# First front of a four-layer hybrid: one of four convolved channel groups on VectorE, vectors in three packs, edges turned ahead of the convolution, first parts reloaded in pieces

## The chip, the cores and the metric

The kernel runs on one NeuronCore of a Trainium2 chip. A core has TensorE (PE, matrix products), VectorE (DVE), ScalarE (ACT), GpSimd (POOL) and SyncE (SP, which here issues nearly all DMAs), each with an instruction stream of its own. The metric is the device time of one execution in microseconds (us); the median of three runs is compared.

## The reference

Four layers work on x of 4 images of 32 x 32 tokens with 256 channels, in float32. Layer 0 is the one that the change touches. For each image:

```python
x = _layernorm(src, ln1_g, ln1_b)
x = x @ w_in + b_in                                  # 256 -> 512 channels
x = conv3x3_depthwise(x, conv_w, padding='SAME') + conv_b
x = gelu(x).reshape(B, L, 512)                       # L = 1024
dt_raw, Bm, Cm = split(x @ w_x, [16, 16 + 64])
dt = softplus(dt_raw @ w_dt + dt_bias)
# h[t] = exp(dt[t] * A) * h[t-1] + dt[t] * x[t] * Bm[t];  y[t] = sum_n h[t] * Cm[t]
y = scan(...) + x * D_skip
out = layernorm(y) @ w_out + b_out                   # and src is added
```

(The call of the convolution is abbreviated; it has one 3 x 3 filter for each of 512 channels.) Layer 1 is a small convolution block. Layer 2 is an attention over tokens whose mask comes from a list of 69,632 edges (source and destination token; only pairs inside the 1024 tokens count), then a mixture of 8 experts. Layer 3 is a second state-space scan (16 states instead of 64), then another mixture of experts.

## The kernel before

**The scans.** Both state-space layers are cut into units of 128 partitions (states x channels) by 1024 time steps: 256 units for each image in layer 0, 64 in layer 3, 1280 in all. The generator `scans` (L364) writes them out in the order `SCANS`: images of layer 0 come ahead of the layer-3 images that depend on them. A unit needs its decay `dA` (a broadcast load of dt from DRAM, `load` L430, then an exponential on ACT, `decay` L443), its input `ps_rep` (a product of a selection matrix with `S`, the bfloat16 parts of dt * x, `first` L453), a product with B on VectorE, the scan itself on VectorE, a product with C on POOL (tile `h`), and a sum over states on TensorE (`pair` L468). `S` is loaded for each 128 channels by `chunk` (L385), which for a new image also loads B and C as `rows`. Loads, decays and inputs are written a few units ahead; `h` has five buffers and `ps_rep` two.

**The stages beside them.** All other work is a list of stages (`STAGES`): four fronts (layer 0 up to dt, x and B, C), four middles (end of layer 0, layers 1 and 2, start of layer 3), four lasts. Each is a generator. `run` (L560) writes two half units of the scan, then lets the current stage go on for some steps, by a clock: `Metered` adds up an estimated cost of every instruction by engine, and the stage goes on only while no engine's sum exceeds VectorE's. So the order of all instructions is fixed when the program is written, by these costs, and the POOL operations count in it.

**The first front.** The first unit needs the first 128 channels of front 0, so `chunk(0)` calls `need` (L525), which writes out stage steps until they are ready. Between two steps it takes one step of `mask_work`, the generator `setup`. That one makes the tables of A (`scan_setup` L321), then the mask (`mask_prepare`: edges loaded, turned by TensorE, turned to addresses, sorted on VectorE so that the valid ones come first, 64 of each partition; the largest count decides in a branch whether more must be sorted), then the scatters: 64 DMAs of POOL, each of which clears one mask entry of each partition, then four branches on POOL for counts above 64. In the scan one step of `mask_work` is taken for each unit.

Before that, `load_vectors` (L196) loads all bias, gain and filter vectors in two packs of rows (96 and 48), each row by a DMA on SP's queue, and turns them by TensorE into columns.

In `front` (L709) the four groups of 128 channels go one after the other (`inward` L737): two matmuls of 512 columns for the input product, evacuated by ACT into a padded image of 34 x 34; nine diagonal matrices made by ACT from the filter; two halves of nine matmuls each (`ps_cv`); gelu on ACT. Then `steps` (L589) follows: for the first 128 channels `linear` and `soft` (softplus on ACT), `rows(1)` (B and C), `add`, `split`, `low` (three bfloat16 parts) and `store`. `prepare`, which folds weights of later layers, follows at the end of front 0.

Of the kernel before, what the change touches and what calls it, by code (L numbers as in the profile page):

```python
# [53 lines left out]
        ("L0_conv_conv_b", 4), ("L0_conv_dt_bias", 4), ("L0_conv_D_skip", 4), ("L0_conv_ln2_g", 4),  # L54
        ("L0_conv_ln2_b", 4), ("L1_conv_b1", 1), ("L1_conv_g1", 1), ("L1_conv_be1", 1),
        ("L1_conv_m1", 1), ("L1_conv_v1", 1), ("L1_conv_b2", 1), ("L1_conv_g2", 1),
        ("L1_conv_be2", 1), ("L1_conv_m2", 1), ("L1_conv_v2", 1), ("L2_attn_bq", 2),
        ("L2_attn_bk", 2), ("L2_attn_bv", 2), ("L3_attn_b_in", 8), ("L3_attn_b_conv", 4), ("L3_attn_b_dt", 4),
    ),
    (("L2_ffn_b1", 16), ("L3_ffn_b1", 32)),  # L60
)

# [70 lines left out]
class Hybrid:  # L133
    def __init__(self, ctx, tc, a, out):
        self.ctx, self.tc, self.nc, self.a = ctx, tc, tc.nc, a
        self.out = out.rearrange("b h w c -> (b h w) c")
        nc = self.nc
        self.const = const = ctx.enter_context(tc.tile_pool(name="const", bufs=1))
        self.dram = ctx.enter_context(tc.tile_pool(name="dram", bufs=1, space=DRAM))

        self.ident = const.tile([P, P], F32, name="ident")
        make_identity(nc, self.ident)
        self.identb = const.tile([P, P], BF16, name="identb")
        nc.vector.tensor_copy(self.identb, self.ident)

        order = const.tile([P, NEXP], I32, name="order")
        nc.gpsimd.iota(order, pattern=[[-1, NEXP]], base=NEXP, channel_multiplier=0)
        self.order = const.tile([P, NEXP], F32, name="orderf")
        nc.vector.tensor_copy(self.order, order)
        self.eps = {}  # L150
        for e in (1e-5, 1e-3):
            self.eps[e] = const.tile([P, 1], F32, name=f"eps{len(self.eps)}")
            nc.vector.memset(self.eps[e], e)

        self.x0 = const.tile([P, TB, C], F32, name="x0")
        nc.sync.dma_start(self.x0, self.image(a["x"].rearrange("b h w c -> (b h w) c"), 0))
        self.w_in0 = self.weight(const, "L0_conv_w_in", 2)
        for _ in self.norm(const, self.x0, TB, self.x0, "ln0"):
            pass

        self.blocks = const.tile([P, P], F32, name="blocks")
        make_block_diagonal(nc, self.blocks, 4)
        self.states = {0: 64, 3: 16}
        self.mem = {}
# [31 lines left out]
    def load_vectors(self):  # L196

        nc, a = self.nc, self.a
        self.vec = {}
        with self.tc.tile_pool(name="vstage", bufs=1) as sp, self.tc.tile_pool(  # L200
            name="vpsum", bufs=1, space=PSUM
        ) as pp:
            for n, pack in enumerate(VEC_PACKS):
                rows = sum(k for _, k in pack)
                stage = sp.tile([rows, P], F32, name=f"vstage{n}")
                r = 0
                for name, k in pack:
                    src = a[name]
                    if name == "L0_conv_conv_w":
                        src = src.rearrange("i j u (k p) -> (i j u k) p", p=P)  # L210
                    elif len(src.shape) == 2:
                        src = src.rearrange("e (k p) -> (e k) p", p=P)
                    else:
                        src = src.rearrange("(k p) -> k p", p=P)
                    nc.sync.dma_start(stage[r : r + k, :], src)
                    r += k
                ps = pp.tile([P, rows], F32, name=f"vps{n}")
                nc.tensor.transpose(ps, stage, self.ident[:rows, :rows])
                cols = self.const.tile([P, rows], F32, name=f"cols{n}")
                nc.vector.tensor_copy(cols, ps)  # L220
                r = 0
                for name, k in pack:
                    self.vec[name] = cols[:, r : r + k]
                    r += k
# [96 lines left out]
    def scan_setup(self, stage, name, n):  # L321
# [8 lines left out]
        flat = self.a[name].rearrange("(u g) n -> u (g n)", g=G)  # L330
        for k in range(0, units, P):
            m = min(P, units - k)
            raw = stage.tile([m, P], F32, name=f"Ar{k}_" + name)
            nc.sync.dma_start(raw, flat[k : k + m, :])
            turned = stage.tile([m, P], F32, name=f"At{k}_" + name)
            nc.vector.tensor_copy(
                turned.rearrange("u (n g) -> u g n", g=G), raw.rearrange("u (g n) -> u g n", n=n)
            )
            ps = self.early("ps_A")
            nc.tensor.transpose(ps[:, :m], turned, self.ident[:m, :m])  # L340
            nc.scalar.activation(cols[:, k : k + m], ps[:, :m], AF.Exp)
# [17 lines left out]
        return cols, spread, collect  # L359
# [4 lines left out]
    def scans(self, mp, psum):  # L364
# [20 lines left out]
        def chunk(k):  # L385

            if k >= len(units):
                return
            scan, d, c, i, j = units[k]
            if (c, i, j) != (0, 0, 0):  # L390
                return
            n = self.states[scan[0]]
            self.need(scan, d)
            if d == 0:
                bct = self.mem["bc", *scan]
                pair = []
                for t in range(2):
                    x = mp.tile([P, L], F32, tag=f"rows{t}", name=f"rows{t}", bufs=2)
                    nc.sync.dma_start(
                        x, bct[t * n : (t + 1) * n, :].unsqueeze(1).to_broadcast([n, P // n, L])  # L400
                    )
                    pair.append(x)
                rows[scan] = pair
            S = mp.tile([3 * 32, 4, L], BF16, tag="S", name="S", bufs=2)
            for s in range(3):
                nc.sync.dma_start(
                    S[32 * s : 32 * s + 32, :, :],
                    self.mem["parts", *scan, d][s].rearrange("(j p) t -> p j t", p=32),
                )
            chunks[scan, d] = S  # L410

# [85 lines left out]
        for k in range(4):  # L497
            load(k)
# [26 lines left out]
    def need(self, scan, d):  # L525

        late = False
        while ("parts", *scan, d) not in self.ready:
# [3 lines left out]
            for _ in range(SCATTERED if self.sorted else 1):  # L532
                next(self.mask_work, None)
        if late:

            self.clock.update(dict.fromkeys(self.clock, max(self.clock.values())))
# [23 lines left out]
    def run(self):  # L560
# [3 lines left out]
        self.alone = False  # L564
        nc, tc = self.nc, self.tc
        with tc.tile_pool(name="scan", bufs=1) as mp, tc.tile_pool(
            name="scps", bufs=1, space=PSUM
        ) as psum, tc.tile_pool(name="sdps", bufs=1, space=PSUM) as side, tc.manual_schedule():
            self.side_psum(side)
            self.mask_work, self.sorted = self.setup(), False  # L570
# [18 lines left out]
    def steps(self, fp, key, w, src, chunks, bias, u, between=None):  # L589
# [65 lines left out]
        if between is not None:  # L655
# [4 lines left out]
            for item in ahead:  # L660
                soft(item)
            yield from between
# [46 lines left out]
    def front(self, b):  # L709
# [3 lines left out]
        with tc.tile_pool(name=f"f{b}", bufs=1, side="right") as op:  # L713
# [4 lines left out]
            with tc.tile_pool(name=f"fa{b}", bufs=1, side="right") as fp:  # L718
# [8 lines left out]
                pads = [fp.tile([P, 34, 34], F32, name=f"pad{i}") for i in range(2)]  # L727
                for i in range(2):
                    nc.gpsimd.memset(pads[i], 0.0)
# [6 lines left out]

                def inward(item):  # L737
                    d, g, k = item
                    pad = pads[d % 2]
                    if g < 0:  # L740
# [10 lines left out]
                        )  # L751
                        if h == 0:
# [32 lines left out]
                items = []  # L785
                for d in range(DC):
                    items += [(d, -1, 0), (d, -1, 1)]
                    items += [(d, g, k) for g in range(2) for k in range(3)]
                yield from self.pipe(items, inward, cost=2.3)
            with tc.tile_pool(name=f"fb{b}", bufs=1, side="right") as fp:  # L790
# [215 lines left out]
    def mask_prepare(self):  # L1006
# [16 lines left out]
        with tc.tile_pool(name="mprep", bufs=1) as mp:  # L1023
# [15 lines left out]
            yield from [None] * 8  # L1039
# [6 lines left out]
            yield from [None] * 4  # L1046
            for a, rawf in enumerate(rawfs):
# [5 lines left out]
                yield  # L1053
# [21 lines left out]
            ps = self.early("ps_c")  # L1075
            nc.tensor.transpose(ps[:1, :P], cnt, self.ident)
            top = mp.tile([1, 1], F32, name="top")
            nc.vector.tensor_reduce(top, ps[:1, :P], AX.X, ALU.max)
            more = mp.tile([1, len(SCATTERS)], F32, name="more")
            for i, (first, _) in enumerate(SCATTERS):  # L1080
                nc.vector.tensor_scalar(more[:, i : i + 1], top, float(first), None, ALU.is_gt)
            nc.vector.tensor_copy(self.more, more)
            order = mp.tile([P, ne], F32, name="sorted")
            few = SCATTERS[0][1]
            nc.vector.memset(order[:, few:], 0.0)
# [9 lines left out]
            yield  # L1095
# [7 lines left out]
            yield  # L1103
# [3 lines left out]
        self.sorted = True  # L1107
# [724 lines left out]
    def setup(self):  # L1832
        with self.tc.tile_pool(name="prep", bufs=1) as st:
            yield
            self.tables = {}
            for scan, name, n in ((0, "L0_conv_A_log", 64), (3, "L3_attn_A_log", 16)):
                self.tables[scan] = self.scan_setup(st, name, n)
                yield
        yield from self.mask_prepare()
# [35 lines left out]
def hybrid_kernel(tc, a, out):  # L1875
    with ExitStack() as ctx:
        k = Hybrid(ctx, tc, a, out)
        k.load_vectors()
# [38 lines left out]
```

## Time and profile before

| what | value |
|---|---|
| median of 3 runs | 6605.04 us (6598.39 to 6610.3) |
| profiled execution | 6610.56 us, its span 6608.8 us |
| VectorE busy | 5140.0 us, 78% |
| GpSimd busy | 3642.9 us, 55% |
| TensorE busy | 5331.1 us, 81%, at a mean granted clock of 0.83 |
| first scan on VectorE starts | 152.63 us |
| unit 256, 512, 1024 start their scan | 1243.9, 2365.2, 4667.3 us |
| last unit starts its scan | 6168.3 us |

A span is the time from the first to the last instruction of the program. The time of a run lies 1.8 us above it. VectorE's 1280 units take most of its time (scan 2.28 us, product with B 1.21 us each); what lies ahead of the first unit has no unit under it. The lines of the profile in the prediction give start and length in us, the engine, the line of the program, the operation with its tiles, the number of instructions, and in brackets how long the engine had been idle and which engine or DMA released it. `ps_cv` is the convolution, `ps_in` the input product, `ps_e` the turned edges, `ps_c` the turned count of edges, `ps_x` the product with w_x, `ps_dt` that with w_dt. A float32 matmul is recorded as two. Line L124 is that of the recording helper, so tiles tell operations apart.

### The profile page before, as it was taken

How to read it: one execution, taken by the hardware profiler on the slowest of the kernel's cores; microseconds unless marked ns; L12 is line 12 of the kernel's file. 1: busy time of each engine (PE TensorE's matmuls, PEld its weight loads, DVE VectorE, ACT ScalarE, POOL GpSimd, SP SyncE). 2: the span in 40 equal slices, each digit the busy share in tenths (PEclk: the TensorE clock that was granted, in tenths of full speed). 3: DMA queues.
4: the chain of work that ended last, by engine and by line, in shares of the span. 5: the costliest groups of instructions: out<-in, count | busy, mean ns of one | idle time of the engine just before them, and what ended most of it. 6: DMA issues, size and time to landing. Idle time of an engine off the chain costs nothing. (4 is left out here: it accounts for less than half of the span.)

```text
span 6608.8 us, 59799 instructions
## 1 busy us (share of the span) xinstructions
PE 5331.1 (81%) x20236; PEld 2161.6 (33%) x20320; DVE 5140.0 (78%) x4310; ACT 3438.2 (52%) x4113; POOL 3642.9 (55%) x1793
## 2 busy tenths in 40 slices
PE   6667868679797568979689779898699688978979
PEld 2022312222342022234145232243255222524656
DVE  3978989988799997889889987898999971248411
ACT  3346566345477334557558445477487344245411
POOL 2857677755458665545856665556756651055200
PEclk8667868689798579979789789898699789877989
DMA  2454555643355566335645664345555750156221
GB/s 103 145 161 159 175 165 163 192 141 113 109 167 173 183 169 152 112 119 179 190 143 170 196 157 129 107 143 174 185 164 163 198 135 15 45 144 159 72 64 35
DMA packets 348113, 936.91 MB, mean 142 GB/s; under 512 B 37140, under 2 KB 119648, under 8 KB 346144
## 3 DMA queue, kind: packets, MB, share of 16 engines
q1 hardware_dynamic: 345616, 930.35, 46.3%
q0 software_dynamic: 2128, 2.13, 0.2%
q8 instruction: 172, 2.82, 0.2%
q14 instruction: 197, 1.61, 0.1%
HBM read 842.59 MB, written 93.95 MB: 142 GB/s over the span
## 5 line engine op out<-in xcount | busy, mean ns | idle before, releaser
L124 POOL TENSOR_TENSOR h<-h,rows 128x1024 f32<-128x1024 f32 x1280 | 3029.7, 2369 | 1948.9 <-DVE h L124 1736.3
L124 DVE TENSOR_TENSOR_SCAN h<-dA,ps_rep 128x1024 f32<-128x1024 f32 x1280 | 2923.9, 2284 | 169.3 <-issue 31.2
L124 DVE TENSOR_TENSOR ps_rep<-ps_rep,rows 128x1024 f32<-128x1024 f32 x1280 | 1552.8, 1213 | 254.0 <-PE ps_rep L124 253.7
L124 ACT ACTIVATE dA<-dA,A_L_conv_A_log 128x1024 f32<-128x1024 f32 x1024 | 1149.8, 1145 | 598.6 <-DMA dA<-dt 554.5
L124 PE MATMUL ps_rep<-S,spread_L_conv_A_log 96*128 96x512 bf16 x2048 | 762.1, 462 | 715.3 <-DVE h L124 694.5
L124 PE MATMUL ps_y<-h,collect_L_conv_A_log 128*32 128x512 f32 x4096 | 795.5, 759 | 70.4 <-POOL h L124 69.9
L124 PE MATMUL ps_h<-xTm,we 128*128 128x512 f32 x1536 | 717.2, 606 | 1.4 <-DVE tb L124 1.4
L124 PE MATMUL ps_e<-we,h_m 128*128 128x256 f32 x3072 | 699.3, 380 | 2.3 <-ACT h_m L124 2.3
L124 ACT ACT_TABLE_LOAD x501 | 642.8, 1283 | 52.0 <-PE ps_h L124 38.6
L124 PEld LDWEIGHTS <-spread_L_conv_A_log 96*128 96x128 bf16 x2048 | 160.7, 103 | 1489.7 <-DVE h L124 1195.1
L124 PEld LDWEIGHTS ps_e<-we,h_m 128*128 128x128 f32 x3072 | 579.9, 190 | 146.3 <-issue 45.5
L124 DVE SCALAR_TENSOR_TENSOR tb<-ps_e,cw,tb 128x256 f32<-128x256 f32 x512 | 220.7, 474 | 408.0 <-PE ps_e L124 407.6
L124 ACT ACTIVATE h_m<-ps_h,cols 128x512 f32<-128x512 f32 x384 | 260.4, 687 | 487.6 <-PE ps_h L124 484.8
L124 ACT ACTIVATE p<-ps_sc 128x512 f32<-128x512 f32 x432 | 234.4, 595 | 470.5 <-PE ps_sc L124 320.0
L124 PEld LDWEIGHTS ps_h<-xTm,we 128*128 128x128 f32 x1536 | 292.4, 194 | 338.5 <-issue 294.1
L124 ACT ACTIVATE dA<-dA,A_L_attn_A_log 128x1024 f32<-128x1024 f32 x256 | 290.5, 1146 | 199.5 <-DMA dA<-dt 164.8
L124 PE MATMUL ps_at<-p,v 128*32 128x512 f32 x1024 | 359.9, 610 | 37.8 <-ACT p L124 25.2
L124 PE MATMUL ps_rep<-S,spread_L_attn_A_log 96*128 96x512 bf16 x512 | 184.4, 448 | 177.0 <-DVE h L124 166.1
L124 PE MATMUL ps_sc<-qT,kT 32*128 32x512 f32 x864 | 249.3, 648 | 30.7 <-issue 22.9
L124 PE MATMUL ps_at<-p,ones 128*32 128x512 f32 x1024 | 271.9, 610 | 0.0
L124 PE MATMUL ps_cv<-pad,diag 128*128 128x512 f32 x576 | 262.0, 597 | 0.0
L124 PEld LDWEIGHTS ps_y<-h,collect_L_conv_A_log 128*32 128x32 f32 x4096 | 109.8, 119 | 458.5 <-issue 237.1
(327 smaller groups left out, 4916.1 us busy)
## 6 DMA issues: line engine op xcount, KB each, us to landing
dA<-dt SPq DMA_DIRECT2D x1280, 512.0 KB
we<-in_L_ffn_W_dram SPq DMA_DIRECT2D x64, 512.0 KB
parts<-parts SPq DMA_DIRECT2D x64, 384.0 KB
S<-parts SPq DMA_DIRECT2D x96, 256.0 KB
dt<-sp_r SPq DMA_DIRECT2D x64, 256.0 KB
y<-yo SPq DMA_DIRECT2D x128, 128.0 KB
y_back<-y SPq DMA_DIRECT2D x64, 256.0 KB
we<-in_L_ffn_w_dram SPq DMA_DIRECT2D x64, 256.0 KB
```

The lines of the kernel that those rows point to most:

```text
L124: return got(*args, **kw)
```

## The change

Five edits belong together.

1. `BY_VECTOR = (3,)`: in front 0 the convolution of channel group 3 is done by VectorE (`beside`): one multiplication and eight multiply-adds of 128 x 1024 over windows of its own padded image. Its input product is the first of the four; its gelu (`activate`) comes after all groups.
2. The vectors come in three packs. The first, with what front 0 needs, is loaded and turned ahead of the norm; the two others are loaded in `setup`, behind the edges and front 0's weights, ahead of the tables' raw data.
3. The edges are loaded first in `setup` and turned ahead of the convolution. Sorting is written before the count is known; count, branch and addresses (`where`) wait until the first softplus is written (`self.ahead`). `need` now ends with a loop that writes `mask_work` up to the end of this part (`self.sorted`), so scatters begin with the scan.
4. For the first `S`, six DMAs are issued by ACT, the first quarter ahead of the rest, and the first `dA` is loaded ahead of `rows`.
5. `scan_setup` is a generator: its loads are all issued first.

```diff
+BY_VECTOR = (3,)
@@ __init__
         self.w_in0 = self.weight(const, "L0_conv_w_in", 2)
+        self.vec = {}
+        first = self.load_vectors(const, 0)
         for _ in self.norm(const, self.x0, TB, self.x0, "ln0"):
             pass
+        with tc.tile_pool(name="vpsum", bufs=1, space=PSUM) as pp:
+            self.turn_vectors(0, first, pp.tile([P, P], F32, name="vps0"))
@@ chunk
+            S = mp.tile([3 * 32, 4, L], BF16, tag="S", name="S", bufs=2)
+
+            def load_parts(js, queue):
+                for s in range(3):
+                    queue.dma_start(
+                        S[32 * s : 32 * s + 32, js, :],
+                        self.mem["parts", *scan, d][s].rearrange("(j p) t -> p j t", p=32)[:, js, :],
+                    )
+
+            if k == 0:
+                load_parts(slice(0, 1), nc.scalar)
+                load_parts(slice(1, 4), nc.scalar)
+                load(0)
             if d == 0:
...
+            if k:
+                load_parts(slice(0, 4), nc.sync)
@@ need
+        while not self.sorted:
+            next(self.mask_work)
@@ steps
             for item in ahead:
                 soft(item)
+            self.ahead = True
             yield from between
@@ front
+                vector = () if b else BY_VECTOR
+                pads = [fp.tile([P, 34, 34], F32, name=f"pad{i}") for i in range(2 + len(vector))]
...
+                def beside(d, pad):
+                    to = u[:, d, :].rearrange("p (h w) -> p h w", w=32)
+                    for k in range(9):
+                        i, j = divmod(k, 3)
+                        window = pad[:, i : i + 32, j : j + 32]
+                        w = vec["L0_conv_conv_w"][:, k * DC + d : k * DC + d + 1]
+                        if k == 0:
+                            nc.vector.tensor_scalar(to, window, w, None, ALU.mult)
+                        else:
+                            nc.vector.scalar_tensor_tensor(to, window, w, to, ALU.mult, ALU.add)
+
+                def activate(d):
+                    nc.scalar.activation(
+                        u[:, d, :], u[:, d, :], AF.Gelu_apprx_tanh,
+                        bias=vec["L0_conv_conv_b"][:, d : d + 1],
+                    )
+                    nc.sync.dma_start(self.keep(("u", *key, d), [P, L]), u[:, d, :])
...
+                        if d in vector:
+                            if h == 1:
+                                beside(d, pad)
+                            return
...
+                items = [(d, -1, h) for d in vector for h in range(2)]
                 for d in range(DC):
-                    items += [(d, -1, 0), (d, -1, 1)]
-                    items += [(d, g, k) for g in range(2) for k in range(3)]
+                    if d not in vector:
+                        items += [(d, -1, 0), (d, -1, 1)]
+                        items += [(d, g, k) for g in range(2) for k in range(3)]
                 yield from self.pipe(items, inward, cost=2.3)
+                for d in vector:
+                    activate(d)
@@ mask_prepare
+            for r in range(0, few, 8):
+                largest(r)
+            while not self.ahead:
+                yield
             ps = self.early("ps_c")
             nc.tensor.transpose(ps[:1, :P], cnt, self.ident)
...
-        self.sorted = True
@@ setup
+            masks = self.mask_prepare()
+            next(masks)
+            stages = [self.load_vectors(st, n) for n in (1, 2)]
             self.tables = {}
+            tables = [
+                self.scan_setup(st, name, n) for name, n in (("L0_conv_A_log", 64), ("L3_attn_A_log", 16))
+            ]
+            for t in tables:
+                next(t)
+            yield
+            yield
+            for t in tables:
+                next(t)
                 yield
+            for n in (1, 2):
+                self.turn_vectors(n, stages[n - 1], self.early("vps"))
+            yield
+            yield from masks
+        self.sorted = True
         yield from self.scatter()
```

## The prediction

> **What bounds the kernel now.** The slices by tenths say where to look: VectorE (DVE) is 9 tenths busy from about 150 us to 5,600 us, and the first 150 us hold no scan. The chain that ended last is of no use here: it reaches back only to 5,606 us, and the change ends before that. So I read the timeline of each engine over the first 400 us. TensorE first (start, length, engine, line, operation, count, idle before and its releaser):
>
> ```profile
> 65.52 0.37 PE L124 MATMUL ps_c<-ident,cnt 128*1 128x128 f32 x1 [6.49 <-DVE cnt L124]
> 65.69 9.36 PE L124 MATMUL ps_cv<-pad,diag 128*128 128x512 f32 x18
> ...
> 112.75 7.04 PE L124 MATMUL ps_x<-u,w_L_conv_w_x 128*16 128x512 f32 x16
> 119.72 1.98 PE L124 MATMUL ps_dt<-dtr,w_dt 16*128 16x512 f32 x4
> 121.63 3.70 PE L124 MATMUL ps_x<-u,w_L_conv_w_x 128*128 128x512 f32 x8
> 128.81 5.40 PE L124 MATMUL ps_x<-u,w_L_conv_w_x 128*128 128x512 f32 x8 [3.48 <-ACT bct L124]
> 150.25 1.87 PE L124 MATMUL ps_rep<-S,spread_L_conv_A_log 96*128 96x512 bf16 x4 [16.04 <-DMA S<-parts]
> ```
>
> From 26.7 to 112.75 us TensorE is the path: four convolved groups, broken once by a wait for the edge count. After that the path is a chain over all engines, and it ends in a load. VectorE beside it:
>
> ```profile
> 79.11 0.71 DVE L1089 MATCH_REPLACE8 lin<-sorted,lin 128x544 f32<-128x544 f32 x1
> 84.50 0.45 DVE L124 TENSOR_SCALAR lin<-sorted 128x544 f32<-128x544 f32 x1 [4.68 <-issue]
> ...
> 126.53 0.69 DVE L124 SCALAR_TENSOR_TENSOR sp_e<-ps_dt,sp_e 128x512 f32<-128x512 f32 x1 [40.35 <-ACT sp_l L124]
> ...
> 137.89 1.46 DVE L124 TENSOR_TENSOR parts<-sp_x,parts 128x512 bf16<-128x512 f32 x2
> 151.29 1.23 DVE L124 TENSOR_TENSOR ps_rep<-ps_rep,rows 128x1024 f32<-128x1024 f32 x1 [11.95 <-PE ps_rep L124]
> 152.63 2.29 DVE L124 TENSOR_TENSOR_SCAN h<-dA,ps_rep 128x1024 f32<-128x1024 f32 x1
> ```
>
> It idles 40 us before 126.53, and the 4.68 us before 84.50 are the branch over the second sort. The first scan, 152.63, is where the 1280 units begin. The DMA issues between, on SP's queue:
>
> ```profile
> 138.63 1.10 SPq L648 DMA_DIRECT2D parts<-parts  x2
> 139.83 1.53 SPq L399 DMA_DIRECT2D rows<-bc  x2
> 142.49 1.30 SPq L406 DMA_DIRECT2D S<-parts  x3
> 143.83 33.37 SPq L438 DMA_DIRECT2D dA<-dt  x12
> ```
>
> Last, GpSimd (POOL) at the end of the mask's scatters, and the busy times from 152 to 321 us (PE, PEld, DVE, ACT, POOL, clock, DMA share, GB/s):
>
> ```profile
> 320.40 1.00 POOL L124 DMA_INDIRECT mask_dram<-zero,where  x1 [0.17 <-issue]
> 321.41 2.37 POOL L124 TENSOR_TENSOR h<-h,rows 128x1024 f32<-128x1024 f32 x1
> 330.03 2.36 POOL L124 TENSOR_TENSOR h<-h,rows 128x1024 f32<-128x1024 f32 x1 [6.25 <-issue]
> ```
> ```profile
> 152.00:321.00 169.00, 109.12 (x260) 14.84 (x262) 155.64 (x95) 72.50 (x77) 153.40 (x94) 0.62 0.46 148
> ```
>
> A unit costs POOL 2.36 us for h, and with a scatter 0.17 + 1.00 + 0.02 more: 3.55 us. VectorE needs 1.21 + 2.29 us and gaps: 3.54 us. While scatters run, both are full.
>
> **What the Trainium skill says.** "Runtime: NRT & Kernel Launch", Instruction fetch mechanics: a taken branch out of the fetched window waits for a DMA of the target page. The trace agrees: 4.68 us on DVE, 6.25 us on POOL at its first branch. "DMA: Bandwidth & Descriptors", Issuing engines are not separate DMA queues: queues share 16 engines, a second issuer saves issue time only. No run here has shown it yet for ACT's queue. "TensorE: Matmul & The Clock Gate", The HAM clock gate: an idle PE is throttled. The 18 matmuls after the gap took 9.36 us, 0.52 each, against 0.434 (15.62 / 36) elsewhere.
>
> **The change, step by step.** *Removed from TensorE:* one convolution, 36 records, 15.62 us; the wait for cnt with its transpose, 6.86; the slow restart, 18 x (0.52 - 0.434) = 1.5. Sum 24.0 us. The edge transposes (2 x 0.77) only move.
>
> *Added ahead of the convolution.* In the built order the A tables now stand behind two weight loads, four edge loads and 21 vector loads on SP. After the pause at 3.98 us (ends 6.36), I count 0.42 + 0.50 + 4 edge loads 1.9 + 19 x 0.295 + 0.8 and the wait for w_in until 7.61: their issue ends at 17.4 against 15.78, so 1.6 us late. Everything through the tables follows (At copy 17.49 to 19.1, second table 24.28 to 25.9). Two vector transposes (0.70 us, "vps" rows 0.39 and 0.31) then stand before ps_in. First ps_in: 26.7 to about 28.9. End of convolution: 112.75 - 24.0 + 2.2 = 91.0 us, so 21.7 us earlier.
>
> *Moved to VectorE:* nine operations of 128x1024. The skip of back0 is the same operation at 1.26 us (median): 9 x 1.26 = 11.3 us. They start when this group's input is evacuated (about 33 us) and end near 45; edges 1.5, cnt 8.3 and sort 12.6 us (from the old rows) end near 67, 24 us before they are missed. I cost them at nothing; without that cover they would be 11.3 us. The gelu of this group (1.15 us on ACT for 1024 columns) follows the last half group; ps_x needs it only as the fourth of its chunks, 2.6 us after the convolution, while it is done after about 2.0: nothing. ACT loses a group's nine diagonals, 2.8 us off the path. One more pad and the clearing of sorted (1.05 and about 0.5 us) go to an idle POOL. The four mask fills leave SP at about 18 us instead of 47.4; behind them on SP stands only the first u store, some 30 us later, while four fills took about 25 us to land (DMA share 0.37 from 50 to 75 us): hidden.
>
> *The count, moved.* The transpose of cnt now stands behind ps_dt and half of ps_x (12.6 us after the convolution, from 121.63 + 3.70 - 112.75), and on VectorE top, the branch and where stand ahead of the softplus additions. So: 13.0, + 0.9 to compare, + 4.7 branch, + 1.7 for where = 20.4 us, where the additions began at 13.8. They last 5.7 us; the casts that follow were waiting in part for bct (until 22.1) before, so the stall passes on only as 3.6 us: last low part 30.2 after the convolution instead of 26.6. Behind it: parts store, S. Bounds: 1 us if the branch is nearly free, 6 if it costs POOL's 6.25.
>
> *First loads.* S comes on ACT's queue, a quarter first, and dA goes ahead of rows. Before, S waited 7.8 us from issue to ps_rep behind 1 MB of rows. With parts landed at 33.4 (2.76 us after issue, as before), three issues 1.3 and about 2 to 3 us to land: ps_rep at 37 after the convolution, before 37.5. Rows, now behind 0.5 MB of dA, should land then too. ACT's six issues, 2.6 us, stand ahead of its first exponential, which so ends by 37.2, with ps_rep. So the reload returns the 3.6 us and about 0.5 more (bounds -2 to +2.5). First scan: 152.6 - 21.7 - 0.5, about 130.4 us: 22.2 us gained.
>
> *The scatters, moved.* Before, 22 of 64 were done by 140 us, on an idle POOL. Now the first two stand before the scan, and in the built order units 0 to 61 carry the others; the sequence behind (four branches, the rest of the first front's additions, then prepare) stands about 11 units later. Up to unit 42 both kernels are alike. From there 11 units go at 3.55, as they would anyhow. But then POOL is the bound: from h of unit 42 (321.4) to the last low part (385.9) it takes 64.5 us, h 14 x 2.36, additions, branches, with hardly a gap, and prepare's loads stand behind that part on SP. The same stretch, units 53 to 66, now holds nine scatters: 9 x 1.17 = 10.5 us. Afterwards the order has only the stage shifted by 11, then 5 units, is the same from unit 518 on, and the shift vanishes in units without stage work (3.54 us each near 500). So 10.5 us are paid back. Bounds: 0, if the lag is drained under prepare's own waits; 26 + 10, if all 22 scatters and the forced request for the second S (unit 59, formerly 52) are paid in full.
>
> Sum: - 22.2 + 10.5 = -11.7 us. Against the profiled run (6610.56 us, span 6608.8) that is 6598.9; the median of the runs is 6605.04, so 6593.
>
> **Rivals.** *All hidden* (22%): POOL's nine scatters cost nothing, since prepare leaves VectorE waiting for weights anyway (7.3 us for ps_b). For it: lag is 0.1 us by unit 56. Against: prepare itself stands behind POOL's last low part. 6605 - 22 = 6583. *Less won at the start* (22%): the count does not do what its place says; branches on DVE, ACT and PE in the chain cost up to 6.25 us, and the tables come later still. -22 + 6 + 10.5: 6599 or so. *Slower* (9%): POOL saturation in full at units 42 to 66. The second S is requested at unit 59 with two fronts' additions forced into one place (10 us), VectorE waits in order for their casts, and 22 scatters cost 26 us, with about 15 more of additions no longer under slack: 51 - 22 = +29, 6634. It decides when the price passes 35 us (22 + 13). Against: POOL's and VectorE's periods are level (3.55 and 3.54), so scatters alone cost nothing until something else is queued.
>
> **How the numbers follow.** The likeliest case, 6593, has 45%; two fifths of it lies beyond the bound of 0.2% (13 us, about what a measurement of this kernel tells from no change). With "all hidden" that gives faster 44%; same 46%, from the rest and "less won"; slower 10% with the slower rival. The range 6577 to 6609 holds the three cases that are not slower, each with 6 us of its own for the clock and the runs' spread (6598 to 6610); the likeliest alone would be 6585 to 6601.
>
> **What would show it.** Right: convolution ends near 91 us without a gap on PE, the nine vector operations end before 50, a VectorE gap of some 4.7 us before where, now after 100 us, first scan near 130, unit 66 late by 10 us against its place. Wrong: a gap on PE before the convolution (tables), a first scan past 135, unit 518 more than 17 us or less than 7 us earlier than now, or differing lengths after it though the order is the same.

## The result: slower, and the profile after

The changed kernel takes 6629.12 us (median of 7 runs, 6625.16 to 6634.69), the kernel before beside it 6606.54 us (7 runs, 6598.39 to 6614.51). The ratio is 1.0034, 95% interval 1.0022 to 1.0045. The profiled execution took 6628.92 us with a span of 6627.2; before they were 6610.56 and 6608.8. The forecast was 6593, in a range of 6577 to 6609.

TensorE after, in the order of the timeline (columns as before: start, length, engine, line, operation, count, idle before and its releaser). The helper that records the operations is now line 128:

```profile
91.95 7.04 PE L128 MATMUL ps_x<-u,w_L_conv_w_x 128*16 128x512 f32 x16
...
104.36 0.27 PE L128 MATMUL ps_c<-ident,cnt 128*1 128x128 f32 x1
108.01 6.67 PE L128 MATMUL ps_x<-u,w_L_conv_w_x 128*128 128x512 f32 x8 [3.37 <-ACT bct L128]
133.35 1.04 PE L128 MATMUL ps_rep<-S,spread_L_conv_A_log 96*128 96x512 bf16 x2 [18.67 <-DMA S<-parts]
140.59 1.01 PE L128 MATMUL ps_rep<-S,spread_L_conv_A_log 96*128 96x512 bf16 x2 [6.20 <-DMA S<-parts]
```

The convolution ends at 91.95 us instead of 112.75, and no wait for the edge count stands in it. But the first ps_rep now has two matmuls where it had four, and the next two wait 6.20 us more for the rest of S. VectorE after:

```profile
34.55 0.75 DVE L128 TENSOR_SCALAR u<-pad,cols 128x1024 f32<-128x1024 f32 x1 [3.66 <-ACT pad L128]
35.34 10.53 DVE L128 SCALAR_TENSOR_TENSOR u<-pad,cols,u 128x1024 f32<-128x1024 f32 x8
...
111.10 0.44 DVE L128 TENSOR_SCALAR lin<-sorted 128x544 f32<-128x544 f32 x1 [5.53 <-issue]
...
120.75 1.46 DVE L128 TENSOR_TENSOR parts<-sp_x,parts 128x512 bf16<-128x512 f32 x2
...
135.76 2.29 DVE L128 TENSOR_TENSOR_SCAN h<-dA,ps_rep 128x1024 f32<-128x1024 f32 x1
141.64 1.23 DVE L128 TENSOR_TENSOR ps_rep<-ps_rep,rows 128x1024 f32<-128x1024 f32 x1 [3.59 <-PE ps_rep L128]
142.98 2.29 DVE L128 TENSOR_TENSOR_SCAN h<-dA,ps_rep 128x1024 f32<-128x1024 f32 x1
```

The nine vector operations take 0.75 + 10.53 us and end at 45.9. The branch is the gap of 5.53 us. The first scan begins at 135.76 instead of 152.63, 16.9 us earlier; the second follows 7.22 us later, not 3.52, so only 13.2 us are left of it. The loads behind this, first SyncE's queue and then ScalarE's:

```profile
121.50 1.10 SPq L672 DMA_DIRECT2D parts<-parts  x2
122.70 0.59 SPq L459 DMA_DIRECT2D dA<-dt  x1
123.39 1.46 SPq L424 DMA_DIRECT2D rows<-bc  x2
125.66 23.66 SPq L459 DMA_DIRECT2D dA<-dt  x7
```
```profile
125.71 7.43 ACTq L410 DMA_DIRECT2D S<-parts  x6
133.19 2.19 ACT L128 ACTIVATE dA<-dA,A_L_conv_A_log 128x1024 f32<-128x1024 f32 x2 [11.70 <-DMA S<-parts]
```

S can be issued once parts has landed, at 125.7 us; dA's first load and both rows are already in flight by then. The six issues span 7.43 us, but that is mostly waiting: a single one takes 0.31 to 0.65 us, 2.74 together (the first line gives the shortest, median and longest in ns), and the fifth and the sixth come late:

```profile
L410 ACTq DMA_DIRECT2D S<-parts x6: 309/467/646, 125.7 to 132.8; - x6
129.03 0.32 ACTq L410 DMA_DIRECT2D S<-parts  x1
132.83 0.31 ACTq L410 DMA_DIRECT2D S<-parts  x1
```

In the records of the trace each DMA of these two queues reports its landing on one of eight semaphores, which the program takes in turn over both queues, and a new DMA waits until the one before on the same semaphore has landed. The fifth piece of S so waited 1.1 us for a rows load (landed at 129.0 us), the sixth 3.5 us for the second piece of S (landed at 132.8); its own data landed at 140.5, and the second unit's ps_rep started at 140.59. SyncE's dA loads, which read nothing of S, wait for it in the same way (who waits for what: us in total, times, longest):

```profile
SPq L459 <- DMA S<-parts: 3.9, 2, 2.9
```

ScalarE's first exponential stands behind the six issues. GpSimd at the end of the scatters:

```profile
399.99 1.01 POOL L128 DMA_INDIRECT mask_dram<-zero,where  x1 [0.16 <-issue]
401.03 2.36 POOL L128 TENSOR_TENSOR h<-h,rows 128x1024 f32<-128x1024 f32 x1
410.09 2.35 POOL L128 TENSOR_TENSOR h<-h,rows 128x1024 f32<-128x1024 f32 x1 [6.70 <-issue]
417.40 2.34 POOL L128 TENSOR_TENSOR h<-h,rows 128x1024 f32<-128x1024 f32 x1 [4.97 <-issue]
```

The last unconditional scatter is at 400, 80 us later than before, and the branches that follow stand directly in front of the last low parts. On VectorE the same place reads:

```profile
380.41 1.23 DVE L128 TENSOR_TENSOR ps_rep<-ps_rep,rows 128x1024 f32<-128x1024 f32 x1 [7.64 <-PE ps_rep L128]
389.57 0.69 DVE L128 TENSOR_TENSOR sp_x<-sp_l,parts 128x512 f32<-128x512 f32 x1 [7.93 <-ACT parts L128]
...
422.73 1.23 DVE L128 TENSOR_TENSOR ps_rep<-ps_rep,rows 128x1024 f32<-128x1024 f32 x1 [8.33 <-PE ps_rep L128]
...
442.25 0.42 DVE L128 TENSOR_TENSOR row_L_conv_b_out<-row_L_conv_b_out,ps_b 128x256 f32<-128x256 f32 x1 [18.29 <-PE ps_b L128]
```

The wait of 7.93 us is for a cast of ScalarE that waits for additions on GpSimd (384 to 389 us). The waits of 7.64 and 8.33 us are for a ps_rep that stands in TensorE's queue behind a sum of h (375.49 and 419.80 us), and GpSimd delivers this h late; in the second case the branches stand ahead of it. That the second S (channels 128 to 255) forces the additions into this place, as the prediction had it, these lines do not show. The wait of 18.29 us is prepare's weight load, which SyncE issues behind the last low part:

```profile
434.28 0.44 SPq L243 DMA_DIRECT2D w_L_conv_w_out<-in_L_conv_w_out_dram  x1
```

In the kernel before, prepare's wait at this place was 7.31 us, and waits of 4.33, 6.36 and 5.32 us stood ahead of it.

**Where the time went.** A unit of the scan is one scan instruction on VectorE, so counting them gives the start of each unit. The table is worked out from those starts: us later (+) or earlier (-) than in the profiled execution of the kernel before, at five units. The last column is the median of the runs against the median of the kernel before that ran beside it. The lower rows are the experiments, by number.

| kernel | unit 0 | unit 16 | unit 80 | unit 256 | unit 512 | median |
|---|---|---|---|---|---|---|
| changed | -16.9 | -13.1 | +11.1 | -0.1 | +25.4 | +22.6 |
| 1 count early | -19.0 | -15.1 | -6.3 | -15.9 | -13.3 | -19.3 |
| 2 before, all scatters in the scan | +0.2 | +0.5 | +23.2 | +13.2 | +18.9 | +11.7 |
| 3 changed, no vector group | -1.0 | +2.1 | +25.4 | +13.5 | +33.4 | +29.5 |
| 4 changed, old reload | -17.7 | -17.6 | +7.0 | -4.6 | +19.1 | +16.8 |
| 5 changed, scatter priced 0 | -17.6 | +9.4 | +36.4 | +1.3 | +5.0 | +6.2 |
| 6 count early, old reload | -23.2 | -23.3 | -17.8 | -26.8 | -23.8 | -21.0 |
| 7 count early, S first on SP | -24.2 | -23.9 | -13.5 | -22.9 | -19.7 | -20.2 |
| 8 before, stage held at 256-261 | +2.3 | +2.3 | +2.8 | +2.4 | +18.1 | +16.1 |
| 9 before, stage held at 256-263 | -0.2 | -0.2 | +1.8 | +0.6 | +10.2 | +9.2 |
| 10 before, vector group alone | -13.1 | -13.1 | -0.5 | -10.5 | -7.7 | -9.8 |

Read the first row from left to right. The start brings 13 us. Between units 16 and 256 the same 13 us are lost: a stall before unit 80 takes 24, and 11 of them come back. Then, between 256 and 512, where nothing of the change stands, another 25.5 us go. From 512 on the order of instructions is that of before again, and unit 512 tells the median within 8 us in every row. Each row is one execution, and whole executions of one kernel differ by up to 25 us (the kernel before: 6594 to 6618), so differences of a few us between rows are not resolved. The five kernels whose order behind unit 256 is that of before (1, 5, 6, 7 and 10) all lose 2.6 to 3.7 us from there to 512: about 3 us of every figure for this stretch belong to the one execution of before.

### The profile page after: what moved, and what is told of

It reads as the page before. It is cut to its first block, busy times and chain, and to the rows that moved or that the text cites. A ratio compares the mean times of both kernels' runs of the same rounds, so it can differ in the third digit from the quotient of the medians.

```text
span 6627.2 us, 59719 instructions
## 1 busy us (share of the span) xinstructions
PE 5319.9 (80%) x20201; PEld 2145.6 (32%) x20285; DVE 5149.0 (78%) x4319; ACT 3429.3 (52%) x4099; POOL 3647.7 (55%) x1795
## 5 line engine op out<-in xcount | busy, mean ns | idle before, releaser
L128 DVE TENSOR_TENSOR_SCAN h<-dA,ps_rep 128x1024 f32<-128x1024 f32 x1280 | 2924.1, 2284 | 163.5 <-issue 30.3
L128 PE MATMUL ps_cv<-pad,diag 128*128 128x512 f32 x540 | 245.1, 595 | 0.0
```

Of the source, the lines that this page charges most:

```text
L128: return got(*args, **kw)
```

## The experiments

The theory after this reading: the gain at the start is real, and the loss was bought with the 20 scatters that went into the scan (22 stood ahead of it before, 2 now) because the count stands behind the first softplus.

**1. The count early.** The changed kernel, its count not held:

```diff
-            while not self.ahead:
-                yield
+            yield from [None] * 9
```

> The changed kernel with one edit: the count's transpose is not held until the first softplus is done but issued after nine steps of the pipe, in the middle of the second convolved group on TensorE. In the built order 18 scatters then stand before the first unit (2 in the changed kernel, 22 in the one before). Theory (the gain at the start carries one to one, and the loss comes from the 22 scatters moved into the scan, about 38 us between units 48 and 512): the branch leaves the chain after the convolution, the last low part ends 3.6 us earlier, first scan near 132 us; four scatters more than before in the scan cost about 5 us; sum 6629 - 3.6 - 32 = about 6594. Rival (the loss of 38 us has another source among the edits, such as the reload or the vector group's stores and loads): only the 3.6 us of the chain are won, about 6625.

Measured: 6589.53 us (11 runs) against 6608.79, ratio 0.9975, interval 0.9966 to 0.9984; faster than both kernels. GpSimd's timeline in this kernel, with the scatters ahead of the first unit:

```profile
75.91 1.20 POOL L128 DMA_INDIRECT mask_dram<-zero,where  x1 [67.71 <-DVE where L128]
78.57 0.98 POOL L128 DMA_INDIRECT mask_dram<-zero,where  x1 [1.46 <-DMA mask_dram<-zero,where]
...
119.61 0.97 POOL L128 DMA_INDIRECT mask_dram<-zero,where  x1 [2.47 <-DMA mask_dram<-zero,where]
```

Eighteen of them, mostly 2.4 us apart because each waits for the one before, all on an idle engine. First scan 133.6 (expected 132), and 15.1 us of gain at unit 16 are still 13.3 at unit 512. This one place in the order is worth 6629 - 6590 = 39 us (38.7 at unit 512), of which the chain at the start is 2.

**2. All scatters in the scan, nothing else.** The kernel before:

```diff
-SCATTERED = 1
+SCATTERED = 0
```

> The kernel before with SCATTERED = 0: all 64 scatters stand in the scan, everything else at the start stays. Theory: first scan unchanged at 152.6 us, and the loss of the changed kernel appears without its other edits: 38 us for 22 scatters, so 6606.5 + 38 = about 6645, with the stall at units 59 to 67 and then a smaller loss up to unit 512. The prediction's own sum (nine scatters of 1.17 us in the stretch where GpSimd is full): 6617. Rival (another edit is the source): 6607 to 6610.

Measured: 6620.48 us (21 runs) against 6608.79, ratio 1.0018, interval 1.0011 to 1.0024. That is 11.7 us, not the theory's 38: the prediction's own sum (10.5) fits here. The stall, now around units 60 to 70, is there all the same, on VectorE:

```profile
403.83 2.22 DVE L124 TENSOR_TENSOR sp_x<-sp_l,parts 128x512 f32<-128x512 f32 x1 [8.71 <-ACT parts L124]
...
462.43 0.42 DVE L124 TENSOR_TENSOR row_L_conv_b_out<-row_L_conv_b_out,ps_b 128x256 f32<-128x256 f32 x1 [20.39 <-PE ps_b L124]
```

23 us at unit 80, but 13.2 at unit 256: ten of them come back, perhaps because a stall leaves the stages behind it with less to wait for (not tested). So the theory in its first form fell: all scatters in the scan cost 12 to 13 us, which leaves the changed kernel's second loss, behind unit 256, open. In this kernel that loss is 5.7 us.

**3. No vector group.** The changed kernel:

```diff
-BY_VECTOR = (3,)
+BY_VECTOR = ()
```

> The changed kernel with BY_VECTOR = (): all four groups are convolved on TensorE again, all else stays. Theory (a start that is later moves every unit): the convolution ends 15.6 us later, first scan near 151 us, 6629 + 15.6 = about 6645. Rival (the time at the start is hidden behind what stands at units 59 to 67): within 4 us of 6629.

Measured: 6638.28 us (5 runs), ratio 1.0055, interval 1.0041 to 1.0068. The first scan is 15.9 us later than in the changed kernel, as the group's price says; at unit 256 it is 13.5, at unit 512 8.0, in the medians 9.2, and 14 by the two ratios (1.0055 and 1.0034). So the gain of the group is not hidden. Whether it carries one to one or a third of it is lost between units 256 and 512, as these two executions have it, the whole times do not decide.

**4. The old reload.** The changed kernel, with S on SyncE's queue in one piece behind rows, and all four dA loads after it:

```diff
-            if k == 0:
-                load_parts(slice(0, 1), nc.scalar)
-                load_parts(slice(1, 4), nc.scalar)
-                load(0)
...
-            if k:
-                load_parts(slice(0, 4), nc.sync)
+            load_parts(slice(0, 4), nc.sync)
...
-        for k in range(1, 4):
+        for k in range(4):
             load(k)
```

> The changed kernel with its reload undone: S comes on SP's queue in one piece behind rows, then the four dA loads. Theory (ACT's six issues took 7.4 us[...] and the second piece came 3.6 us late for the second unit): first scan within 1 us of 135.8, second scan 3.6 us earlier, 6629 - 3.6 = about 6625. The prediction's step (the reload returns 4 us): first scan near 140, about 6633. Rival (the reload changes the order of transfers later, too, and carries the loss): below 6615.

Measured: 6625.59 us (6 runs), ratio 1.0031, interval 1.0019 to 1.0043. Its TensorE and VectorE at the first units:

```profile
132.55 1.87 PE L128 MATMUL ps_rep<-S,spread_L_conv_A_log 96*128 96x512 bf16 x4 [17.91 <-DMA S<-parts]
```
```profile
134.94 2.29 DVE L128 TENSOR_TENSOR_SCAN h<-dA,ps_rep 128x1024 f32<-128x1024 f32 x1
137.15 1.21 DVE L128 TENSOR_TENSOR ps_rep<-ps_rep,rows 128x1024 f32<-128x1024 f32 x1
138.46 2.29 DVE L128 TENSOR_TENSOR_SCAN h<-dA,ps_rep 128x1024 f32<-128x1024 f32 x1
```

Here SyncE issues S at 125.75, no later than ScalarE did, and all of it has landed when the changed kernel has its first quarter (132.55 against 133.35); the second scan follows at once, 4.5 us ahead of the changed kernel's. SyncE's three issues took 1.30 us together: the DMAs before them on their semaphores had landed. So at the start the reload in pieces is a loss of 4.5 us, where the prediction had a gain of 4. The medians are 3.5 us apart, as the theory expected, but a difference of that size lies within the intervals.

**5. The scatters priced at nothing.** What follows from the planner's price alone? In the changed kernel:

```diff
-            "indirect_dma_start": lambda **_: 1.0,
+            "indirect_dma_start": lambda **_: 0.0,
```

> The changed kernel with the planner's price of a scatter set from 1.0 to 0: the 62 scatters stay in the scan, but the rest of the first front and prepare are no longer held back by them; in the built order the front's last additions stand at units 16 to 20 rather than 64, and from unit 259 the order is that of the kernel before. Theory A (the loss of 35 to 40 us is the later place of the stage, not GpSimd's time for the scatters): first scan 135.8 as in the changed kernel, no stall at unit 59, unit 512 about 15 us earlier than before, about 6592. Theory B (GpSimd's time for 22 more scatters is itself the price, 12 us as with all scatters in the scan of the kernel before): about 6603. Rival (the scatters' traffic or waits cost it all): 6625 or more.

Measured: 6613.72 us (14 runs) against 6607.56, ratio 1.0008, interval 1.0000 to 1.0016. That is between theory B and the rival, and better than the changed kernel by 15 us, with the same scatters in the scan. Theory A expected no stall; it is there, and larger: 36.4 us late at unit 80, against 11.1. At unit 256 it stands where the changed kernel stands (+1.3 and -0.1), so up to there the earlier stage bought nothing; 18.9 us are lost from the first unit on, with the same 62 scatters, but what part of it is theirs was not separated. Behind 256, in the order of the kernel before, it loses 3.7 us instead of 25.5. The second loss goes with the order, not with GpSimd's time.

**8 and 9. The order behind unit 256 by itself.** In the changed kernel the first image's middle stage stands four to five units later against the scan than before, on VectorE up to unit 462. The kernel before with the stage held a little does only this (n counts half units):

```diff
-                for _ in range(TICKS):
+                for _ in range(0 if 512 <= n < 524 else TICKS):
```

> The kernel before, with the stage held for units 256 to 261 and nothing else: from unit 270 to 512 its program then is that of the changed kernel (its middle stage stands four to five units later against the chunks of the scan), with the scatters and the start of the kernel before. Theory (the 25 us that the changed kernel loses between units 256 and 512 are the price of this alignment): unit 256 at 1244 as before, unit 512 about 25 us later than before, about 6630. Rival (they are a backlog from the scatters or from the loads at the start): unit 512 within 5 us of before, about 6609.

Measured: 6623.62 us (14 runs) against 6607.56, ratio 1.0026, interval 1.0018 to 1.0033. Unit 256 at +2.4, unit 512 at +18.1: 15.7 us from the order alone. The windows view over units 256 to 512, for the kernel before, this one, and the changed one (columns: stretch, its length, busy time of PE, PEld, DVE, ACT, POOL, clock, DMA share, GB/s):

```profile
1243.90:2365.20 1121.30, 877.54 (x3519) 305.01 (x3541) 990.34 (x768) 586.11 (x694) 688.77 (x322) 0.81 0.47 149
```
```profile
1246.30:2383.30 1137.00, 875.14 (x3519) 301.13 (x3541) 994.17 (x767) 580.43 (x689) 686.49 (x322) 0.80 0.46 147
```
```profile
1243.80:2390.60 1146.80, 883.20 (x3519) 301.20 (x3541) 997.19 (x770) 582.33 (x690) 694.79 (x326) 0.80 0.46 150
```

The work is the same but for a few us. What VectorE's busy time leaves over grows from 131.0 to 142.8 and 149.6 us. TensorE's clock (0.81, 0.80, 0.80) does not carry it: TensorE's busy time is not greater in the held kernel, and experiment 3 has 0.81 in this stretch, too, and takes 20 us longer there. One of the places, in the kernel before and then in the held one:

```profile
1709.46 0.69 DVE L124 TENSOR_TENSOR y_at<-ps_wo,xa 128x512 f32<-128x512 f32 x1 [0.85 <-PE ps_wo L124]
1712.90 0.69 DVE L124 TENSOR_TENSOR y_at<-ps_wo,xa 128x512 f32<-128x512 f32 x1 [2.75 <-PE ps_wo L124]
```
```profile
1740.94 0.69 DVE L124 TENSOR_TENSOR y_at<-ps_wo,xa 128x512 f32<-128x512 f32 x1 [5.60 <-PE ps_wo L124]
1743.61 0.69 DVE L124 TENSOR_TENSOR y_at<-ps_wo,xa 128x512 f32<-128x512 f32 x1 [1.98 <-PE ps_wo L124]
```

Summed over the stretch, waits for ps_wo are 5.4 us longer, for parts 4.1, for sp_l 2.7. The stage's instructions stand in VectorE's queue among scan instructions. That a few units' shift leaves TensorE and ScalarE less time before VectorE needs their results is the reading of these waits; it was not tested apart.

The same shift can be read off the other kernels, by comparing the order of VectorE's instructions with that of before. Four kernels have it at four to five units (the changed one, 3, 4 and 8); from unit 256 to 512 they lose 25.5, 19.9, 23.7 and 15.7 us. The five with no shift lose 2.6 to 3.7.

The ninth holds the stage for two units more (512 <= n < 528), which is about where it stands in experiment 2:

> As the eighth kernel, but the stage is held for units 256 to 263, so that the middle stage stands six to seven units later than in the kernel before, where it also stands when all 64 scatters are in the scan. Theory (the price is one of phase between the stage and the chunks of the scan, not of lateness: that kernel lost only 6 us between units 256 and 512): unit 512 about 6 us later than before, about 6613. Rival (the later the stage, the more it costs): 20 us or more, 6628 and above.

Measured: 6616.05 us (21 runs) against 6606.82, ratio 1.0017, interval 1.0010 to 1.0023. 9.6 us between units 256 and 512, 9.2 in all: less than with the shorter hold, where the rival expected 20 or more. So the price does not grow with lateness; that the phase between stage and scan sets it fits, and is not shown further. Experiment 2, at about the same shift, lost little there too (5.7 us), though in units 256 to 272, where the ninth kernel lost 2.2. Of the three waits named, those for ps_wo (9.6 us in the ninth kernel, 9.9 in the eighth, 4.5 before) and sp_l (7.0, 7.0, 4.3) are as long in both held kernels; only those for parts (7.5, 10.7, 6.6) are shorter in the ninth. Not all of the changed kernel's 25.5 us is covered: 9.0 of them fall into units 256 to 272, where its order and the held kernel's still differ (3.1 there). What makes four to five units dearer than six to seven stays open.

**6 and 7. Count early, with another reload.** The edits of 1 and 4 together:

> The count early (first experiment) and the old reload (fourth experiment) together. If both effects add: 6589.5 - 3.5 = 6586, first scan near 133, second 3.5 us behind it. If the reload's loss was only due to the later place of the chain: no difference from 6589.5.

Measured: 6586.58 us (6 runs) against 6607.56, ratio 0.9971, interval 0.9959 to 0.9983. That is the sum expected if both effects add, though 3 us cannot be told from experiment 1 by whole times. First scan 129.40 (133 expected), 23.2 us earlier than before, and 23.8 us at unit 512: nothing is lost on the way. (This execution, at 6579, was the fastest of the six.) The seventh puts S on SyncE's queue in one piece, ahead of dA and rows:

```diff
             if k == 0:
-                load_parts(slice(0, 1), nc.scalar)
-                load_parts(slice(1, 4), nc.scalar)
+                load_parts(slice(0, 4), nc.sync)
                 load(0)
```

> The count early, and S on SP's queue in one piece ahead of dA and rows. Theory (S landed late since it queued behind 0.5 MB of dA and 1 MB of rows[...]): S lands some 4 us after its issue at 120, rows are then the last, first scan near 130 and the second 3.5 us behind: 6589.5 - 3.5 - 3 = about 6583. Rival (what has to land before the first scan is the same 2 MB in any order): first scan 133 as with the old reload, 6586.

Measured: 6587.35 us (6 runs), ratio 0.9967, interval 0.9954 to 0.9980. First scan 128.5 (the theory had 130), 0.9 us ahead of experiment 6, and 4 us behind it by unit 512: no difference that can be told. That fits the rival: what has to land first is much the same in any order.

**10. The vector group alone.** The kernel before with BY_VECTOR, the third pad, beside, activate and the new list of items, and no other part of the change:

> The kernel before with the vector group alone: the fourth group on VectorE first, the additional pad, its gelu last; vectors in two packs, edges turned during the convolution, count, branch and reload all as before. In the built order the transpose of cnt stands in the middle of the second convolved group, about 57 us, after cnt's 55.5; 16 scatters stand before the first unit, and from unit 259 the order is that of before. Theory (the gain is the group's 15.6 us and the wait for cnt, and the loss was bought with the other edits): convolution ends near 89 us, first scan near 129, six more scatters in the scan cost 4 us; 6607 - 23 + 4 = about 6588. Rival (the edges and tables have to be moved too, as TensorE waits for cnt behind nine vector operations): a gap of 7 us or more on TensorE before cnt's transpose, first scan 137 or later, 6596 or more.

Measured: 6596.99 us (21 runs) against 6606.82, ratio 0.9982, interval 0.9975 to 0.9988. Faster than before, but here the rival was right. TensorE's timeline in this kernel:

```profile
64.32 0.37 PE L125 MATMUL ps_c<-ident,cnt 128*1 128x128 f32 x1 [6.50 <-DVE cnt L125]
64.49 15.62 PE L125 MATMUL ps_cv<-pad,diag 128*128 128x512 f32 x30
```

The wait for cnt stays, 6.50 us, since the edges are turned on TensorE between the groups and VectorE gets them late; the first scan is at 139.5. The 10 us between this kernel and experiment 6 are what the rest of the new start brings (edges turned ahead of the convolution, sorting ahead of the count, vectors in three packs, tables later); 7 of them are the wait that is gone, and the parts were not taken one by one. So of the change the vector group gains and the earlier edges seem to; the place of the count loses, and so does the reload at the start.

## Why the prediction was wrong

Its steps, in its order.

- *Removed from TensorE, 24.0 us, and 2.2 us added ahead:* right within 2 us. First ps_in 28.14 (28.9 forecast), end of the convolution 91.95 (91.0). The terms given for the added loads add up to 16.4 us, not the 17.4 written; the issue ended at 17.1.
- *Moved to VectorE, at nothing:* right. 11.28 us (11.3 forecast), sort done at 68 of 91.95; no wait for it on any engine. Experiment 3 gives the group 15.9 us at the first scan.
- *The count, moved:* right as far as the chain goes. Branch 5.53 us (4.7), last low part done at 122.2, 30.3 after the convolution (30.2). Experiment 1 bought back 2.2 us of it at the first scan. The step missed what this place does far behind.
- *First loads:* wrong in sign. ScalarE's six issues were priced at 2.6 us and did take 2.7, but the waits for earlier landings between them, 4.7 us, were put at nothing, and S in two pieces put a second wait on the path: first scan at 135.8, not 130.4, second unit 3.6 us later again. Experiment 4 shows the reload as a loss of 4.5 us at the second scan. "DMA: Bandwidth & Descriptors", Issuing engines are not separate DMA queues, in the Trainium skill, says that a second issuer saves no more than the time to issue, usually small beside the DMA itself. The traces agree that there was little to win: SyncE's three issues of the whole S took 1.30 us before.
- *The scatters, moved, 10.5 us:* right within 3 us, but in part by luck, as the picture was another. Experiment 2, which adds 22 scatters to the scan, costs 13.2 us by unit 256; the changed kernel loses 13.0 from unit 16 to 256, experiment 5 18.9 from unit 0. On the way the changed kernel stalls for 24 us, as additions, branches and prepare come together, and gets 11 of them back.
- *"Afterwards the order has only the stage shifted ... and the shift vanishes in units without stage work":* this is the step that failed. It was costed at nothing, with no bound. With four to five units of shift 25.5 us went between units 256 and 512; experiment 8 shows 15.7 of that in a kernel with no other edit, and experiment 5 that all but 3.7 goes when the order is restored.

The sum of the missed terms, at unit 512: 9.0 us less won at the start (22.2 forecast, 13.2 there), 2.5 more for the scatters, 25.5 behind unit 256, 37 us in all. The forecast of -11.7 becomes +25.3, and the trace has +25.4; that they agree is no test, since the three terms are read from that same trace. The profiled execution of the kernel before then took 6 us longer from 512 to the last unit, in the same order, which need not be an effect of the change: nine of the ten experiments were 2 to 12 us shorter there, too, and one was 2 us longer.

Of the rivals, "slower" named 6634 and came within 5 us of the time, but by luck, since its mechanism was another: it had 51 us in units 42 to 66, while 24 us were lost by unit 80, 13 for good. "Less won" was half right: the start did bring less, from the reload and not from branches. (Its chance of "faster" does not follow from its cases: two fifths of 45% and 22% make 40%, not 44%.) Of the signs given, "unit 518 less than 7 us earlier" and "a first scan past 135" were the ones that told.

## What to carry to other kernels

When an edit delays a side job in a kernel whose order a planner writes, cost where its followers land for as long as the shift lasts, not only until it is drained: here that stretch lost more than the moved work itself. Do a side job where its engine is idle anyway; in experiment 1, 18 scatters ran on a GpSimd that had nothing else to do, and 20 to 22 more in the scan went with 12 to 19 us of loss. And before splitting a load into more DMAs on another queue, find out which earlier DMA each of them has to wait for: such a wait stands in front of that engine's own work.

## What was not expected of the hardware

- Six DMA issues on ScalarE's queue spanned 7.43 us (7.85 in experiment 1), of which the issues themselves were 2.74; in the rest the queue waited for the landing of earlier DMAs on the same semaphores. On SyncE's queue three issues of the same data took 1.30 us.
- A scatter that follows a scatter starts 2.4 us after it (0.97 us, and 1.44 waiting for the one before); between two h products it took 1.00 us with 0.17 before it.
- The gap at the branch on VectorE was 5.53 us in the changed kernel and 4.47 to 5.58 in all twelve; GpSimd's were 6.70, 4.97, 4.27 and 5.17 us, four times in a row.
